# Attention on one core: part of the exponentials moved from ScalarE to a polynomial on VectorE and GpSimd, and the score product split over two row blocks

## The chip, the cores and the metric

The kernel runs on one core of a Trainium2 chip. The metric is the device time of one execution in microseconds (us). Times are compared as medians of several executions of each kernel on the same chip. The names of engines follow the profile: PE is TensorE (PEld its weight loads), DVE is VectorE, ACT is ScalarE, POOL is GpSimd, SP is SyncE.

## The reference: what is computed

The program is a small network of five stages on x of shape 4 x 1024 x 128, all in float32: half a mixture of experts, a selective state-space layer (S6), half a mixture of experts, and the same again with attention in the middle. Only the attention is changed. With 16 heads of 8 columns and 16 "wavelength channels" it computes, cut to what matters:

```python
cos_pm = jnp.cos(phase_modulators)          # 16 channels x 16 heads
def wl_step(acc, wl):
    cpm, iw = wl
    m = cpm[None, :, None, None]
    scores = jnp.einsum('bhqd,bhkd->bhqk', Q * m, K * m) * SCALE
    scores = scores * jnp.cos(KERR * scores * scores)
    attn = jax.nn.softmax(scores, axis=-1)
    out = jnp.einsum('bhqk,bhkd->bhqd', attn, V)
    return (acc + out * iw, None)
...
combined = acc / WL_CHANNELS
```

KERR is 2.7e-12, so the inner cosine is 1 in float32 for scores of this size. A bound on the scores is computed at run time, and the kernel takes the short way (`attention_small`) when it holds, as it does for these inputs. What is left is, for each of 4 batches x 16 heads x 16 channels, exp(c x s) over a 1024 x 1024 matrix s with a factor c per head and channel, then a product with V and a division by the row sums.

## The kernel before, in words

The stages before and after the attention keep x in SBUF (`x_sb`) and run layer norm, experts and S6 over it. S6 (`s6`, lines 226 to 380) is drawn on below only for what its rows show: there DVE runs a scan with two SBUF inputs (L342) and elementwise steps (L313 to L318), while POOL multiplies hst and c_sb (L353) and copies single columns (L351).

`attention` (L527) makes the factors cc and iw from the phase modulators (through `half_sine`), evaluates the bound, and branches to `attention_small` (L594). That function works head by head, 64 heads u in all (4 batches x 16), and 16 channels wl in each, so 1024 channels, numbered g below:

- `batch(b)` normalises and transposes a batch's rows (`xnt`) and makes V with a column of ones (`vts`), so that the row sums come out of the same product.
- `group(n)` makes q and k of four heads (HG = 4) at once, each head on its own block of 32 partitions; row 0 of a block is reserved for the row maxima (q) and ones (k).
- `score(j, a, i, c)` multiplies one 128-row block against all 1024 columns (L712), two matmuls of 512 columns on the head's one block of 32 rows, into a PSUM tile `s` (two buffers).
- `prepare(u)` is a generator of 16 pieces: eight score tiles whose negated maxima go to `nm` (`maxima`, L726), the maxima transposed into the reserved row of q (L734, L741), then eight score tiles in the other orientation, copied to SBUF as `xs` (`head`, L750). With the maxima in the product, `xs` is the shifted score. One piece of the next head but one is advanced per channel.
- The channel loop (L810): one ACTIVATE takes exp of all 8192 columns of `xs` with the channel's factor (L812) into `p_w` (two buffers). PE multiplies it with V in 64 matmuls (L821), in turn on four blocks of output columns, into `o` (two banks). DVE copies `o` to `os` (L829); PE transposes it back (L842); every second channel DVE copies two transposed channels into `ot` (L846).
- `weigh(u, ot)` runs once a head, in the next head's channel 0: reciprocal, weights, product and sum over channels into `comb` (L757 to L770). `out(b)` projects a finished batch in eight pieces (`project`, L508).

The order is written out by hand for PE and DVE (`tc.manual_schedule`, L794): both engines run their instructions in the order in which the loop issues them. The list `beside` says in which channels of which heads the pieces of `group`, `batch` and `out` are issued. ACT and POOL run in the order of issue too. POOL does nothing during the channel loop.

Of the kernel before, what the change touches and what calls it, by code (L numbers as in the profile page):

```python
# [19 lines left out]
F32 = mybir.dt.float32  # L20
# [23 lines left out]
PI2_1 = 6.28125  # L44
PI2_2 = 0.0019350051879882812
PI2_3 = 2.0 * math.pi - PI2_1 - PI2_2
RSQRT = 1597463007.0
LN_TINY = -87.33654

# [468 lines left out]
    nc.vector.tensor_tensor(xt, xt, k.bo, op=ALU.add)  # L518


HG = 4
NG = H // HG
QQ = 4
QW = L // QQ


def attention(tc, k):  # L527
# [8 lines left out]
    with ExitStack() as ctx:  # L536
# [5 lines left out]
        with (  # L542
            tc.tile_pool(name="at_p", bufs=2) as sb,
            tc.tile_pool(name="at_tr", bufs=2, space=PSUM) as ps_tr,
        ):
            z = half_sine(nc, sb, k.pm, H * WL)
            m = sb.tile([P, H * WL], F32, name="m")
            nc.vector.scalar_tensor_tensor(m, z, -2.0, z, op0=ALU.mult, op1=ALU.mult)
            nc.vector.tensor_scalar(m, m, 1.0, None, op0=ALU.add)
            m_hw = m.rearrange("p (w h) -> p h w", h=H)  # L550
            nc.vector.scalar_tensor_tensor(cc, m_hw, SCALE, m_hw, op0=ALU.mult, op1=ALU.mult)
            nc.vector.tensor_scalar(iw, k.iw, 1.0 / WL, None, op0=ALU.mult)

            pb = ps_tr.tile([1, 2, P], F32, name="pb", tag="tr")
            for j, (w_t, b_t) in enumerate(((k.wq, k.bq), (k.wk, k.bk))):
                w2 = sb.tile([C, C], F32, name="w2")
                nc.vector.tensor_tensor(w2, w_t, w_t, op=ALU.mult)
                pn = ps_tr.tile([P, 1], F32, name="pn", tag="pn")  # L560
# [33 lines left out]
def attention_small(tc, k, cc, iw):  # L594
# [10 lines left out]
    with (  # L605
# [5 lines left out]
        tc.tile_pool(name="as_o", bufs=1, space=PSUM) as ps_o,  # L611
    ):

        wp, bp = [], []
        for x, w_t in (("q", k.wq), ("k", k.wk)):
            w = one.tile([C, NG, HG, 32], F32, name=f"wp_{x}")
            nc.gpsimd.memset(w, 0.0)
            nc.gpsimd.tensor_copy(
                w[:, :, :, 1 : 1 + D], w_t.rearrange("c (g j d) -> c g j d", j=HG, d=D)
            )  # L620
            wp.append(w)
            b_t = one.tile([P, NG], F32, name=f"bp_{x}")
            nc.gpsimd.memset(b_t, 0.0)
            if x == "k":
                for j in range(HG):
                    nc.gpsimd.memset(b_t[32 * j : 32 * j + 1, :], 1.0)
            for j in range(HG):
                nc.sync.dma_start(
                    out=b_t[32 * j + 1 : 32 * j + 1 + D, :],
                    in_=k.b_dram[x].rearrange("(g j d) -> j d g", j=HG, d=D)[j],  # L630
                )
            bp.append(b_t)
        nm = one.tile([P, GT], F32, name="nm")
        vts = []
        for j in range(2):
            vt = one.tile([P, GT, H, D + 1], F32, name=f"vt{j}")
            nc.gpsimd.memset(vt[:, :, :, D : D + 1], 1.0)
            vts.append(vt)
        ob = []
# [5 lines left out]
        xnt, qp, kp, comb, xs = {}, {}, {}, {}, {}  # L645

        def batch(b):

# [5 lines left out]
            for half in range(2):  # L654
                pt = ps_t.tile([P, 4, P], F32, name="pt", tag="tr")
                for i in range(4):
                    t = b * GT + half * 4 + i
                    xn = sb.tile([P, C], F32, name="ln_xn", bufs=4)
# [26 lines left out]
        def group(n):  # L685

            for w, b_t, x, at in zip(wp, bp, "qk", (qp, kp)):
                at[n] = sb.tile([P, L], F32, name=f"{x}p")
                for half in range(2):
                    pq = ps_t.tile([P, 512], F32, name="pq", tag="tr")  # L690
                    nc.tensor.matmul(
                        pq,
                        w[:, n % NG].rearrange("c j d -> c (j d)"),
                        xnt[n // NG][:, ts(half, 512)],
                        start=True,
                        stop=True,
# [9 lines left out]

        def score(j, a, i, c):

            row = slice(32 * j, 32 * j + 32)
            s = ps_s.tile([P, L], F32, name="s")  # L710
            for half in range(2):
                nc.tensor.matmul(  # L712
                    s[:, ts(half, 512)],
                    a[row, ts(i, P)],
# [6 lines left out]
        def maxima(u):  # L721

            n, j = divmod(u, HG)
            row = slice(32 * j, 32 * j + 1)
            for i in range(GT):
                nc.vector.tensor_reduce(  # L726
                    nm[:, i : i + 1], score(j, qp[n], i, kp[n]), AX.X, ALU.max, negate=True
                )
                if i < GT - 1:
                    yield  # L730
            for half in range(2):
                pt = ps_t.tile([P, 4, P], F32, name="pt", tag="tr")
                for i in range(4):
                    nc.tensor.matmul(  # L734
                        pt[row, i, :],
                        nm[:, half * 4 + i : half * 4 + i + 1],
                        k.ident,
                        start=True,
                        stop=True,
                    )  # L740
                nc.vector.tensor_copy(  # L741
                    qp[n][row, ts(half, 512)], pt[row].rearrange("p a b -> p (a b)")
                )
            yield

        def head(u):
            n, j = divmod(u, HG)
            xs[u] = xp.tile([P, GT, L], F32, name="xs")
            for i in range(GT):
                nc.vector.tensor_copy(xs[u][:, i, :], score(j, kp[n], i, qp[n]))  # L750
                yield

        def weigh(u, ot):

# [11 lines left out]
            )  # L766

            if h == 0:
                comb[b] = sb.tile([P, 2, QQ, C], F32, name="comb")
# [24 lines left out]
        with tc.manual_schedule(engines={mybir.EngineType.PE, mybir.EngineType.DVE}):  # L794
            finish(batch(0), group(0), prepare(0))
            ahead = prepare(1)
            next(ahead)
            for u in range(n_heads):
                n, j = divmod(u, HG)
                b, h = divmod(u, H)  # L800

                beside = []
                if j == 2 and n + 1 < B * NG:
                    beside.append((10, 14, group(n + 1)))
                if n % NG == 3 and j == 1 and b + 1 < B:
                    beside.append((4, 9, batch(b + 1)))
                if b > 0 and h == 2:
                    beside.append((2, 10, out(b - 1)))
                ot = sb.tile([P, WL, 2 * QQ, D + 1], F32, name="ot", bufs=1)
                for wl in range(WL):  # L810
                    p_w = xp.tile([P, GT, L], F32, name="p_w")
                    nc.scalar.activation(  # L812
                        p_w.rearrange("p a b -> p (a b)"),
                        xs[u].rearrange("p a b -> p (a b)"),
                        AF.Exp,
                        scale=cc[:, h, wl : wl + 1],
                    )
                    o = ob[wl % 2]
                    for i in range(GT):
                        for r in range(QQ):  # L820
                            nc.tensor.matmul(  # L821
                                o[32 * r : 32 * r + D + 1, 0:QW],
                                vts[b % 2][:, i, h, :],
                                p_w[:, i, ts(r, QW)],
                                start=(i == 0),
                                stop=(i == GT - 1),
                            )
                    os = sb.tile([P, QW], F32, name="os")
                    nc.vector.tensor_copy(os, o[:, 0:QW])  # L829
# [5 lines left out]
                    if wl == WL - 1 and u + 2 < n_heads:  # L835
                        finish(ahead)
                        ahead = prepare(u + 2)
                    next(ahead, None)
                    if wl % 2 == 0:
                        pt = ps_t.tile([P, 4, P], F32, name="pt", tag="tr")  # L840
                    for c in range(2):
# [152 lines left out]
def load_attention(nc, pool, k, a):  # L994
# [8 lines left out]
    get(  # L1003
        "pm",
        [P, WL * H],
        a["L1_attn_phase_modulators"].rearrange("w h -> (w h)").partition_broadcast(P),
    )
    get("iw", [P, WL], a["L1_attn_interference_weights"].partition_broadcast(P))


# [93 lines left out]
```

## Time and profile before

| | |
|---|---|
| three timed runs | 8819.01, 8826.69, 8832.57 us; median 8826.69 us |
| profiled execution, its own time | 8833.98 us |
| its span from first to last instruction | 8832.1 us |
| PE busy / PEld busy | 7823.0 / 3392.0 us |
| ACT busy | 7665.0 us |
| DVE busy | 3262.1 us |
| POOL busy | 608.7 us, all before 1400 us |
| granted TensorE clock, mean | 0.918 |
| channel loop, first to last exponential | 1424.5 to 8640.5 us: PE 6531.9, DVE 2224.9, ACT 7167.5 us busy, clock 0.95 |

How to read the lines that follow. A group of the profile's fifth part is a line of the kernel, the engine, the operation, the tile written and the tiles read, their shapes and the number of instructions; then the busy time of all of them in us and the mean of one in ns; then the idle time of the engine just before them and what ended it. A line of the timeline has the start in us, the duration in us, the engine, line, operation, tiles and number of instructions merged into it, and in brackets the idle time before it. Matmuls are pipelined, so their durations overlap: 64 matmuls of 403 ns fill about 4 us. The spans on POOL are rough.

### The profile page before, as it was taken

Reading aid. Unit: us, or ns where it says so; the run is one execution under the profiler, and the core shown is the slowest. Engines: PE = TensorE matmul, PEld = TensorE weight load, DVE = VectorE, ACT = ScalarE, POOL = GpSimd, SP = SyncE. Lnnn points to the kernel's source line nnn. Section 1 sums busy time; section 2 is a strip of 40 time slices with the busy share of each in tenths; the row PEclk is TensorE's granted clock in tenths of the full one; section 3 lists DMA queues with packets and bytes.
Section 4 is the critical chain, followed back from the end, with each engine's and each line's share of the span. In section 5 each row is a group of like instructions: output and inputs, shape, how many; then the busy total and the mean of one; then the engine's idle time right before and its main releaser. Section 6 shows DMA issues by size and latency. Waiting matters only on the chain. (4 is left out here: it accounts for less than half of the span.)

```text
span 8832.1 us, 164134 instructions
## 1 busy us (share of the span) xinstructions
PE 7823.0 (89%) x76474; PEld 3392.0 (38%) x76474; DVE 3262.1 (37%) x5409; ACT 7665.0 (87%) x1746; POOL 608.7 (7%) x579
## 2 busy tenths in 40 slices
PE   8888887999899998989999999999999999899985
PEld 5222253333333333333333333333333333333333
DVE  6777773323333333323233323223333333323222
ACT  3333325999999999999999999999999999999992
POOL 3444430000000000000000000000000000000000
PEclk9777787999999999999999999999999999999996
DMA  0000000000000000000000000000000000000000
GB/s 18 0 0 0 0 6 4 1 1 1 1 1 1 1 1 1 1 1 1 1 1 1 1 1 1 1 1 1 1 1 1 1 1 1 1 1 1 1 1 16
DMA packets 14326, 19.40 MB, mean 2 GB/s; under 512 B 2986, under 2 KB 12722, under 8 KB 13620
## 3 DMA queue, kind: packets, MB, share of 16 engines
q8 instruction: 609, 9.98, 0.5%
q1 hardware_dynamic: 9316, 6.01, 0.2%
q10 hardware_dynamic: 4304, 2.62, 0.1%
q14 instruction: 97, 0.79, 0.0%
HBM read 6.53 MB, written 2.10 MB: 1 GB/s over the span
## 5 line engine op out<-in xcount | busy, mean ns | idle before, releaser
L812 ACT ACTIVATE p_w<-xs,cc 128x8192 f32<-128x8192 f32 x1024 | 7188.6, 7109 | 48.5 <-DVE xs L750 29.1
L821 PE MATMUL o<-p_w,vt 128*9 128x256 f32 x65536 | 4055.1, 403 | 654.3 <-ACT p_w L812 653.4
L821 PEld LDWEIGHTS o<-p_w,vt 128*9 128x9 f32 x65536 | 1809.4, 95 | 2608.2 <-ACT p_w L812 804.3
L829 DVE COPY os<-o 128x256 f32<-128x256 f32 x1024 | 434.9, 425 | 3595.2 <-PE o L821 3595.2
L712 PE MATMUL s<-kp,qp 32*128 32x512 f32 x2048 | 1026.5, 621 | 0.0
L712 PE MATMUL s<-qp,kp 32*128 32x512 f32 x2048 | 1022.1, 619 | 0.0
L750 DVE COPY xs<-s 128x1024 f32<-128x1024 f32 x512 | 627.1, 1225 | 730.4 <-PE s L712 724.3
L726 DVE TENSOR_REDUCE nm<-s 128x1 f32<-128x1024 f32 x512 | 626.2, 1223 | 647.5 <-PE s L712 647.5
L712 PEld LDWEIGHTS s<-qp,kp 32*128 32x128 f32 x2048 | 343.6, 186 | 491.2 <-issue 486.9
L712 PEld LDWEIGHTS s<-kp,qp 32*128 32x128 f32 x2048 | 344.7, 186 | 471.7 <-issue 467.0
L842 PEld LDWEIGHTS pt<-ident,os 128*128 128x128 f32 x2048 | 206.2, 141 | 764.1 <-issue 669.0
L354 PE MATMUL yp<-hm,ident 128*128 128x512 f32 x512 | 388.7, 880 | 99.2 <-POOL hm L353 97.7
L842 PE MATMUL pt<-ident,os 128*128 128x128 f32 x2048 | 450.3, 302 | 19.6 <-DVE os L829 9.6
L336 ACT ACTIVATE da<-delta,neg_a 128x512 f32<-128x512 f32 x256 | 182.7, 721 | 291.9 <-DVE hst L342 291.5
L353 POOL TENSOR_TENSOR hm<-hst,c_sb 128x512 f32<-128x512 f32 x256 | 369.9, 1457 | 166.3 <-ACT c_sb L333 113.3
L178 ACT ACTIVATE r<-hp 128x512 f32<-128x512 f32 x160 | 95.5, 597 | 207.9 <-PE hp L176 185.5
L354 PEld LDWEIGHTS yp<-hm,ident 128*128 128x128 f32 x512 | 110.0, 252 | 348.9 <-POOL hm L353 318.0
L340 DVE TENSOR_TENSOR db<-du,bp 128x512 f32<-128x512 f32 x256 | 164.2, 682 | 152.9 <-PE bp L329 152.0
L333 ACT COPY c_sb<-cp 128x512 f32<-128x512 f32 x128 | 74.8, 585 | 166.1 <-PE cp L331 129.0
L342 DVE TENSOR_TENSOR_SCAN hst<-da,last,db 128x512 f32<-128x512 f32 x128 | 192.0, 1540 | 0.0
L180 POOL TENSOR_TENSOR h<-r 128x512 f32<-128x512 f32 x160 | 164.6, 1047 | 201.7 <-ACT r L178 201.3
L342 DVE TENSOR_TENSOR_SCAN hst<-da,db 128x512 f32<-128x512 f32 x128 | 171.1, 1372 | 5.6 <-POOL hm L353 4.4
(176 smaller groups left out, 3102.8 us busy)
## 6 DMA issues: line engine op xcount, KB each, us to landing
x_sb<-in_L_attn_x_dram ACTq DMA_DIRECT2D x4, 512.0 KB
c_w<-in_L_ffn_w_dram SPq DMA_DIRECT2D x4, 512.0 KB
out_dram<-x_sb SPq DMA_DIRECT2D x4, 512.0 KB
c_w<-in_L_ffn_w_stack_dram SPq DMA_DIRECT2D x1, 512.0 KB
c_w<-in_L_ffn_w_stack_dram ACTq DMA_DIRECT2D x1, 512.0 KB
c_ws<-in_L_ffn_ws_dram SPq DMA_DIRECT2D x2, 128.0 KB
c_w_in<-in_L_attn_W_in_dram SPq DMA_DIRECT2D x1, 256.0 KB
c_w_out<-in_L_attn_W_out_dram SPq DMA_DIRECT2D x1, 128.0 KB
```

Source lines behind the costliest of these rows:

```text
L180: nc.gpsimd.tensor_tensor(h, r, r, op=ALU.mult)
L336: nc.scalar.activation(da, delta[:, c, hc], AF.Exp, scale=neg_a[:, c, n : n + 1])
L342: nc.vector.tensor_tensor_scan(hst, da, db, 0.0 if half == 0 else last[:, c, n : n + 1], op0=ALU.mult, op1=ALU.add,)
L353: nc.gpsimd.tensor_tensor(hm, hst, c_sb, op=ALU.mult)
L354: nc.tensor.matmul(yp[c], k.ident, hm, start=(n == 0), stop=(n == NS - 1))
L712: nc.tensor.matmul(s[:, ts(half, 512)], a[row, ts(i, P)], c[row, ts(half, 512)], start=True, stop=True,)
L726: nc.vector.tensor_reduce(nm[:, i : i + 1], score(j, qp[n], i, kp[n]), AX.X, ALU.max, negate=True)
L750: nc.vector.tensor_copy(xs[u][:, i, :], score(j, kp[n], i, qp[n]))
L812: nc.scalar.activation(p_w.rearrange("p a b -> p (a b)"), xs[u].rearrange("p a b -> p (a b)"), AF.Exp, scale=cc[:, h, wl : wl + 1],)
L821: nc.tensor.matmul(o[32 * r : 32 * r + D + 1, 0:QW], vts[b % 2][:, i, h, :], p_w[:, i, ts(r, QW)], start=(i == 0), stop=(i == GT - 1),)
L829: nc.vector.tensor_copy(os, o[:, 0:QW])
L842: nc.tensor.transpose(pt[:, wl % 2 * 2 + c, :], os[:, ts(c, P)], k.ident)
```

## The change

Four edits in `attention_small`, and some that make room for them.

1. *A polynomial for 512 of the 8192 columns.* The ACTIVATE of a channel takes columns 512 to 8191 only. The first 512 (row block 0, columns 0 to 511) are formed as powers of two: `split(g)` scales the scores and clamps them on DVE, and on POOL rounds them, makes the exponent bits and subtracts (four instructions); `power(g)` evaluates a quintic by five scalar_tensor_tensor on DVE, the last of which multiplies by the exponent bits and writes into `p_w`. The quintic is divided by its top coefficient, and V is multiplied by it for these columns (`vtop`, once a head).
2. *One channel ahead.* In channel g the loop issues split(g + 2), then power(g + 1), after the piece of `prepare`. `p_w` of channel g + 1 is claimed there.
3. *Summed last.* The 64 matmuls of o take row blocks 1 to 7 first and block 0, in which the polynomial's columns lie, last.
4. *Two row blocks a head.* HG is 2: q and k of a head stand twice, on two blocks of 32 partitions, and the two matmuls of a score tile use one block each. The maxima are transposed to 64 rows and added, not copied. `group` now runs every second head and copies its weights on POOL each time (64 such copies).

Beside these, `pm` is loaded when attention starts and not with the other weights; `ln_xn` has one buffer instead of four and `comb` one instead of two; `out` is issued in the first head of the next batch.

```diff
-HG = 4
+HG = 2
+SOFT = 512
...
+            pm = sb.tile([P, WL * H], F32, name="pm", bufs=1)
+            nc.sync.dma_start(
+                out=pm, in_=k.pm_dram.rearrange("w h -> (w h)").partition_broadcast(P)
+            )
...
         def score(j, a, i, c):
-            row = slice(32 * j, 32 * j + 32)
             s = ps_s.tile([P, L], F32, name="s")
             for half in range(2):
+                row = slice(64 * j + 32 * half, 64 * j + 32 * half + 32)
...
+            nc.vector.tensor_copy(nm[:, :, 32], nm[:, :, 0])
...
-                nc.vector.tensor_copy(
-                    qp[n][row, ts(half, 512)], pt[row].rearrange("p a b -> p (a b)")
-                )
+                at = qp[n][rows, ts(half, 512)]
+                nc.vector.tensor_tensor(
+                    at, at, pt[rows].rearrange("p a b -> p (a b)"), op=ALU.add
+                )
...
+        def split(g):
+            u, wl = divmod(g, WL)
+            s, c = xs[u][:, 0, 0:SOFT], cc2[:, u % H, wl : wl + 1]
+            r = sb.tile([P, SOFT], F32, name="x_r")
+            nc.vector.tensor_scalar(r, s, c, -127.0, op0=ALU.mult, op1=ALU.max)
+            p = sb.tile([P, SOFT], F32, name="x_p")
+            nc.gpsimd.tensor_scalar(p, r, 1.0, ROUND, op0=ALU.mult, op1=ALU.add)
+            nc.gpsimd.tensor_scalar(p, p, 1.0, -ROUND, op0=ALU.mult, op1=ALU.add)
+            e = sb.tile([P, SOFT], I32, name="x_e")
+            nc.gpsimd.tensor_scalar(
+                e, p, float(1 << 23), 127.0 * (1 << 23), op0=ALU.mult, op1=ALU.add
+            )
+            nc.gpsimd.tensor_tensor(r, r, p, op=ALU.subtract)
+            return e, r, p
+
+        def power(g, e, r, p):
+            p_w[g] = xp.tile([P, GT, L], F32, name="p_w")
+            nc.vector.scalar_tensor_tensor(p, r, EXP2[4], r, op0=ALU.add, op1=ALU.mult)
+            for c in EXP2[3], EXP2[2], EXP2[1]:
+                nc.vector.scalar_tensor_tensor(p, p, c, r, op0=ALU.add, op1=ALU.mult)
+            nc.vector.scalar_tensor_tensor(
+                p_w[g][:, 0, 0:SOFT],
+                p,
+                EXP2[0],
+                e.bitcast(F32),
+                op0=ALU.add,
+                op1=ALU.mult,
+            )
...
+            power(0, *split(0))
+            parts = split(1)
             for u in range(n_heads):
...
-                if j == 2 and n + 1 < B * NG:
+                if j == 0 and n + 1 < B * NG:
                     beside.append((10, 14, group(n + 1)))
...
+                vtop = sb.tile([P, D + 1], F32, name="vtop")
+                nc.vector.tensor_scalar(vtop, vts[b % 2][:, 0, h], EXP2_TOP, None, op0=ALU.mult)
                 for wl in range(WL):
-                    p_w = xp.tile([P, GT, L], F32, name="p_w")
+                    g = u * WL + wl
                     nc.scalar.activation(
-                        p_w.rearrange("p a b -> p (a b)"),
-                        xs[u].rearrange("p a b -> p (a b)"),
+                        p_w[g].rearrange("p a b -> p (a b)")[:, SOFT:],
+                        xs[u].rearrange("p a b -> p (a b)")[:, SOFT:],
                         AF.Exp,
                         scale=cc[:, h, wl : wl + 1],
                     )
                     o = ob[wl % 2]
-                    for i in range(GT):
+                    for i in (*range(1, GT), 0):
                         for r in range(QQ):
+                            soft = i * L + r * QW < SOFT
                             nc.tensor.matmul(
                                 o[32 * r : 32 * r + D + 1, 0:QW],
-                                vts[b % 2][:, i, h, :],
-                                p_w[:, i, ts(r, QW)],
-                                start=(i == 0),
-                                stop=(i == GT - 1),
+                                vtop if soft else vts[b % 2][:, i, h, :],
+                                p_w[g][:, i, ts(r, QW)],
+                                start=(i == 1),
+                                stop=(i == 0),
                             )
...
                     next(ahead, None)
+                    done, parts = parts, split(g + 2) if g + 2 < n_heads * WL else None
+                    if done:
+                        power(g + 1, *done)
```

In the line numbers of the changed kernel, `split` is L768 to L783, `power` L785 to L798, the ACTIVATE L863 and the matmuls of o L873.

More of the change, by code (lines that the diff above doesn't have):

```diff
@@ L46 @@
 PI2_3 = 2.0 * math.pi - PI2_1 - PI2_2
+LOG2E = 1.4426950408889634
+EXP2 = (753.2121929788568, 522.0867097099356, 180.93752180790148, 41.80864617280965,
+        7.287735181996136)
+EXP2_TOP = 0.0013276472167819944
 RSQRT = 1597463007.0
@@ L545, in attention @@
         ):
-            z = half_sine(nc, sb, k.pm, H * WL)
+            pm = sb.tile([P, WL * H], F32, name="pm", bufs=1)
+            nc.sync.dma_start(
+                out=pm, in_=k.pm_dram.rearrange("w h -> (w h)").partition_broadcast(P)
+            )
+            z = half_sine(nc, sb, pm, H * WL)
             m = sb.tile([P, H * WL], F32, name="m")
@@ L614, in attention_small @@
         wp, bp = [], []
-        for x, w_t in (("q", k.wq), ("k", k.wk)):
-            w = one.tile([C, NG, HG, 32], F32, name=f"wp_{x}")
+        for x in "qk":
+            w = one.tile([C, HG, 2, 32], F32, name=f"wp_{x}")
             nc.gpsimd.memset(w, 0.0)
-            nc.gpsimd.tensor_copy(
-                w[:, :, :, 1 : 1 + D], w_t.rearrange("c (g j d) -> c g j d", j=HG, d=D)
-            )
             wp.append(w)
@@ L623, in attention_small @@
             nc.gpsimd.memset(b_t, 0.0)
[L624 to L627, printed above, removed]
+            for blk in range(4):
+                if x == "k":
+                    nc.gpsimd.memset(b_t[32 * blk : 32 * blk + 1, :], 1.0)
                 nc.sync.dma_start(
-                    out=b_t[32 * j + 1 : 32 * j + 1 + D, :],
-                    in_=k.b_dram[x].rearrange("(g j d) -> j d g", j=HG, d=D)[j],
+                    out=b_t[32 * blk + 1 : 32 * blk + 1 + D, :],
+                    in_=k.b_dram[x].rearrange("(g j d) -> j d g", j=HG, d=D)[blk // 2],
                 )
             bp.append(b_t)
-        nm = one.tile([P, GT], F32, name="nm")
+        nm = one.tile([P, GT, 64], F32, name="nm")
+        nc.gpsimd.memset(nm, 0.0)
         vts = []
@@ L638, in attention_small @@
             vts.append(vt)
+        cc2 = one.tile([P, H, WL], F32, name="cc2")
+        nc.vector.tensor_scalar(cc2, cc, LOG2E, None, op0=ALU.mult)
         ob = []
@@ L643, in attention_small @@
             ob.append(o)
-        xnt, qp, kp, comb, xs = {}, {}, {}, {}, {}
+        xnt, qp, kp, comb, xs, p_w = {}, {}, {}, {}, {}, {}
         def batch(b):
@@ L657, in batch @@
                     t = b * GT + half * 4 + i
-                    xn = sb.tile([P, C], F32, name="ln_xn", bufs=4)
+                    xn = sb.tile([P, C], F32, name="ln_xn", bufs=1)
                     nc.vector.tensor_scalar(
@@ L687, in group @@
             for w, b_t, x, at in zip(wp, bp, "qk", (qp, kp)):
+                nc.gpsimd.tensor_copy(
+                    w[:, :, :, 1 : 1 + D],
+                    (k.wq if x == "q" else k.wk)
+                    .rearrange("c (g j o d) -> c g j o d", j=HG, o=1, d=D)[:, n % NG]
+                    .to_broadcast([C, HG, 2, D]),
+                )
                 at[n] = sb.tile([P, L], F32, name=f"{x}p")
@@ L692, in group @@
                         pq,
-                        w[:, n % NG].rearrange("c j d -> c (j d)"),
+                        w.rearrange("c j h d -> c (j h d)"),
                         xnt[n // NG][:, ts(half, 512)],
@@ L723, in maxima @@
             n, j = divmod(u, HG)
-            row = slice(32 * j, 32 * j + 1)
+            rows = slice(64 * j, 64 * j + 64)
             for i in range(GT):
                 nc.vector.tensor_reduce(
-                    nm[:, i : i + 1], score(j, qp[n], i, kp[n]), AX.X, ALU.max, negate=True
+                    nm[:, i, 0:1], score(j, qp[n], i, kp[n]), AX.X, ALU.max, negate=True
                 )
@@ L734, in maxima @@
                     nc.tensor.matmul(
[L735 to L739, printed above, removed]
-                    )
-                nc.vector.tensor_copy(
-                    qp[n][row, ts(half, 512)], pt[row].rearrange("p a b -> p (a b)")
+                        pt[rows, i, :], nm[:, half * 4 + i, :], k.ident, start=True, stop=True
+                    )
+                at = qp[n][rows, ts(half, 512)]
+                nc.vector.tensor_tensor(
+                    at, at, pt[rows].rearrange("p a b -> p (a b)"), op=ALU.add
                 )
@@ L768, in weigh @@
             if h == 0:
-                comb[b] = sb.tile([P, 2, QQ, C], F32, name="comb")
+                comb[b] = sb.tile([P, 2, QQ, C], F32, name="comb", bufs=1)
             nc.vector.tensor_reduce(
@@ L802, in attention_small @@
                 beside = []
-                if j == 2 and n + 1 < B * NG:
+                if j == 0 and n + 1 < B * NG:
                     beside.append((10, 14, group(n + 1)))
-                if n % NG == 3 and j == 1 and b + 1 < B:
+                if n % NG == NG - 2 and j == 1 and b + 1 < B:
                     beside.append((4, 9, batch(b + 1)))
-                if b > 0 and h == 2:
-                    beside.append((2, 10, out(b - 1)))
+                if b > 0 and h == 0:
+                    beside.append((1, 9, out(b - 1)))
                 ot = sb.tile([P, WL, 2 * QQ, D + 1], F32, name="ot", bufs=1)
+                vtop = sb.tile([P, D + 1], F32, name="vtop")
+                nc.vector.tensor_scalar(vtop, vts[b % 2][:, 0, h], EXP2_TOP, None, op0=ALU.mult)
                 for wl in range(WL):
-                    p_w = xp.tile([P, GT, L], F32, name="p_w")
+                    g = u * WL + wl
                     nc.scalar.activation(
-                        p_w.rearrange("p a b -> p (a b)"),
-                        xs[u].rearrange("p a b -> p (a b)"),
+                        p_w[g].rearrange("p a b -> p (a b)")[:, SOFT:],
+                        xs[u].rearrange("p a b -> p (a b)")[:, SOFT:],
                         AF.Exp,
@@ L1002, in load_attention @@
     k.b_dram = {x: a[f"L1_attn_b{x}"] for x in "qk"}
[L1003 to L1007, printed above, removed]
+    k.pm_dram = a["L1_attn_phase_modulators"]
     get("iw", [P, WL], a["L1_attn_interference_weights"].partition_broadcast(P))
```

## The prediction

> **What bounds the kernel now.** I read the totals and the costliest groups first, then the order of time inside one channel, then the groups of POOL, then two places where engines meet.
>
> ```profile
> span 8832.1 us, 164134 instructions
> ...
> L812 ACT ACTIVATE p_w<-xs,cc 128x8192 f32<-128x8192 f32 x1024 | 7188.6, 7109 | 48.5 <-DVE xs L750 29.1
> L821 PE MATMUL o<-p_w,vt 128*9 128x256 f32 x65536 | 4055.1, 403 | 654.3 <-ACT p_w L812 653.4
> ...
> L829 DVE COPY os<-o 128x256 f32<-128x256 f32 x1024 | 434.9, 425 | 3595.2 <-PE o L821 3595.2
> ```
>
> 1024 exponentials fill 7188.6 us and wait 48.5 in all, so ScalarE sets the pace of attention. Its instructions run from 1424.5 to 8640.5 us: 7216 us, **7.05 us a channel**. The other 1616 us (layer norms, experts, S6) are touched only by small set-up edits; 1.9 us lie outside the span (profiled time 8833.98, 7.3 above the median of the runs, 8826.69).
>
> One channel in the timeline (start, duration, engine, line):
>
> ```profile
> 5005.41 1.98 PE L712 MATMUL s<-qp,kp 32*128 32x512 f32 x4
> 5005.55 0.42 DVE L829 COPY os<-o 128x256 f32<-128x256 f32 x1 [2.75 <-PE o L821]
> ...
> 5007.43 1.22 DVE L750 COPY xs<-s 128x1024 f32<-128x1024 f32 x1 [1.46 <-PE s L712]
> ...
> 5008.68 5.14 PE L821 MATMUL o<-p_w,vt 128*9 128x256 f32 x64 [0.93 <-ACT p_w L812]
> ```
>
> After channel g's o, PE makes one score tile (1.98 us), then DVE drains it (1.22). DVE then idles until the next o ends. Nothing in this string feeds the next exponential at once; it has a whole channel of slack.
>
> **What the change removes.** 512 of 8192 columns leave each ACTIVATE. L336's 128x512 takes 721 ns, L812's 128x8192 7109: 0.832 ns a column, so 0.43 us a channel, 436 us in all, and a pace of 6.62 if ScalarE stays the bound. The score tile's two halves move to two row blocks. Where head 0's tile (rows 0 to 31) met head 1's (rows 32 to 63), before the loop, the trace shows what that gives:
>
> ```profile
> 1419.79 1.21 PE L712 MATMUL s<-kp,qp 32*128 32x512 f32 x1
> 1419.98 1.05 PE L712 MATMUL s<-qp,kp 32*128 32x512 f32 x1
> ```
>
> The two tiles' matmuls run side by side. A tile should cost 1.1 us (half of 1.98 plus the drain) instead of 1.98; bounds 1.1 and 2.0.
>
> **What it adds, and where.** In the built program DVE's order in channel g becomes: os(g), score drain, r(g+2), five scalar_tensor_tensor of power(g+1), os(g+1). The last of the five writes the block that the last eight matmuls of o(g+1) wait for; os(g+1) and the next score tile stand behind those on DVE and PE. So a **ring** closes each channel: end of o(g), score, drain, r, power, end of o(g+1). The exponential runs up to a channel ahead and doesn't relax it. The pace is the larger of 6.62 and the ring.
>
> Uncontended: score 1.1; drain 0.04 + 1.22; r 0.43 (L313, a tensor_scalar of 1024, took 669 to 694 ns, L473's of 256 took 296); five power steps at 0.69 (L133, 128x512 with two inputs, 686 ns) and 0.03 between, 3.6; tail 0.74 (64 matmuls took 3.6 at full clock, so eight 0.43, plus 0.23 of latency, and 0.08 from a release to the first matmul, as from the exponential's end at 5008.60). Sum 7.1.
>
> What was hidden and now stands on the ring: per head, weigh (0.94 + 0.29 + 1.22 + 2.08 less 1.0 beside the score tile, 3.5), the maxima's copy, transposes and two adds (0.16 + 0.7 + 2 x 0.69 by L734 and L741, 2.3), per two heads four group steps (0.86 on PE and L698's 0.75 less what overlaps, about 1.0 each; there are twice as many groups), batch and out (20 steps of about 2.5 and 32 of about 2.2, each a short walk between DVE and PE: 120 us over the run), vtop 0.2. Over 16 channels 0.62. The uncontended ring is **7.7 us**, above 7.05 already.
>
> **The port.** POOL does four steps of split(g+2) exactly while DVE does power(g+1): both start from r's end. Both read SBUF. The S6 stage shows such a meeting (DVE's step with two SBUF inputs against POOL's product):
>
> ```profile
> 919.20 1.26 POOL L353 TENSOR_TENSOR hm<-hst,c_sb 128x512 f32<-128x512 f32 x1
> 919.24 2.30 DVE L314 SCALAR_TENSOR_TENSOR sp_z<-sp_w,sp_z 128x1024 f32<-128x1024 f32 x1
> ```
>
> L314 is the kind of step that power adds. Beside hm it took 2.30 us, in four of its eight runs 1.23: it waited to hm's end and then needed 1.08. POOL waits alike: of 256 hm, 54 that began inside a scan took 1.06 from the scan's end against 1.26 alone, and the copy of one column stretched from 0.17 to 1.14. The Trainium skill, "SBUF — State Buffer", section "Who interferes with whom", says that a DVE instruction with two SBUF inputs and a GpSimd one that reads SBUF exclude each other for the whole instruction. Row and rule disagree on price: by the rule as stated the nine steps add in full (with T, below, 0.8 before its wait: 3.45 + 1.26 + 2.4 = 7.1 us); by the rows each step that waited is 0.15 (DVE) or 0.20 (POOL) shorter after it. I take the rows. Since each POOL step waits for its forerunner, as DVE's do, the two alternate: 0.69 + 4 x 0.54 + 1.06 for the subtraction + 3T + 8 hand-overs of 0.03 = 4.15 + 3T.
>
> T, a POOL tensor_scalar of 512 with one input, after its wait, is in no row. Near it:
>
> ```profile
> L180 POOL TENSOR_TENSOR h<-r 128x512 f32<-128x512 f32 x160 | 164.6, 1047 | 201.7 <-ACT r L178 201.3
> ...
> L617 POOL MEMSET wp_q<- 128x512 f32 x1 | 0.5, 524 | 70.3 <-DVEq L582 70.3
> ...
> L618 POOL COPY wp_q<-c_wq 128x128 f32<-128x128 f32 x1 | 0.3, 309 | 0.0
> ```
>
> The copy reads one input: (309 - 100)/128 = 1.63 ns a column over about 0.1 fixed (the memsets of a few columns), 0.94 at 512, 0.74 after a wait. "GPSIMD Engine Reference", section "Engine selection", has one-input work at roughly line rate, which speaks for the change: the memset's 0.52 shows that rate, 0.35 after a wait (an estimate). The ring part is 5.2 by the rule and 6.4 by the row; the ceiling is the two-input cost, 1.06, giving 7.3. I take T = 0.6, nearer the row, since that copy writes runs of eight: 5.95 in place of 3.6.
>
> Ring: 1.1 + 1.26 + 0.43 + 5.95 + 0.74 + 0.62 = **10.1 us**.
>
> **Clock.** PE was granted 0.95 over the loop and busy 6.53 of 7.22 ms; its work would be 5.2 us in 10. From 1400 to 1434 us, with PE on score tiles alone, the grant was half. At half speed score and tail grow by 1.65 us a channel; bounds 0 and 1.65. I take a quarter, 0.4: **10.5 us**.
>
> **Small edits.** pm now loads when attention starts (L473 waited 1.5 us for it; 0 to 5 us once). One ln_xn buffer instead of four ties each transpose to the next (in the 120 us). Weight copies on POOL, 64 of about 0.3, queue between the splits and delay a group step by that, under 20 us. An extra copy of nm, 0.16 a head, is in the 2.3. Total: 1616 + 1.9 + 1024 x 10.5 + 20 = 12,390; I say **12,400 us**.
>
> **Rivals.**
> (a) Alternation as above, 0.76: from T = 0.35 with full clock (9.4: 11,250) to T = 1.06 with the clock mostly low (about 12.0: 13,900).
> (b) The two meet only in part, about half of the 2.4 us, because POOL gets ahead or its steps are short, 0.12: ring 8.9, 10,750. For it: no row shows four POOL steps against five of DVE. Against: both wait for their own forerunner and start together.
> (c) No exclusion for these forms: ring 7.7, 9,520; 0.07. Against: L314 is the same form.
> (d) The other side, 0.05: ScalarE stays the bound at 6.62, 1616 + 2 + 6779 + 20 = 8,420. Mechanism: the ring closes inside the shorter exponential, since power's dependent steps overlap in DVE and POOL's fall beside the drain, which reads PSUM. It decides where the ring is below 7.05; the uncontended sum is 0.65 above that, and below 6.62 the full gain appears. If the score tile also failed to shorten, the ring would gain another 0.9.
>
> That the polynomial's work isn't done as said isn't open: the instructions stand in the program.
>
> **Numbers.** Likeliest 12,400. Range 10,500 to 13,800: it takes in most of (a) and the greater part of (b), and leaves out (c), (d), the foot of (b) and the top of (a), about 0.2. A measurement can tell about 0.2% from no change. Faster by more 0.05 (d), within 0.01, slower 0.94.
>
> **What would show it.** ACT idle before L863 of about 3.5 us a channel, released by PE o; power's steps (L788 to L791) with means near 1.1 us instead of 0.69; POOL's L776 to L782 stretched likewise; PE waiting for p_w L791 inside each o; score tiles near 1.1 us. Wrong if L790 means 0.69 (then (c)), if ACT's idle stays under 0.1 us a channel (then (d)), or if L776's own time is far from 0.6.

## The result, and the profile after

| | before | changed |
|---|---|---|
| median (range) of 4 runs each | 8822.85 us (8812.24 to 8832.57) | 11696.75 us (11682.87 to 11707.53) |
| ratio, 95% interval | | 1.3257 (1.3234 to 1.328) |
| profiled execution: own time, span | 8833.98, 8832.1 | 11691.15, 11689.3 |
| first to last exponential of the channel loop | 7237 us, 7.07 a channel | 10,106 us, 9.87 a channel |
| outside the loop | 1595 us | 1583 us |
| granted TensorE clock in the loop | 0.95 | 0.83 |

The change makes the kernel a third slower, and all of the difference, 2869 us, lies in the loop over the channels. (The loop of before really ends at 8661.5 us. The 8640.5 of the prediction, and of the table of before, was 21 us short, so the prediction's "outside" was 21 too large.)

The groups of the changed kernel's page, with the same columns as before:

```profile
L863 ACT ACTIVATE p_w<-xs,cc 128x7680 f32<-128x7680 f32 x1024 | 6855.9, 6699 | 3250.1 <-PE o L873 2886.8
...
L776 POOL TENSOR_SCALAR x_p<-x_r 128x512 f32<-128x512 f32 x1024 | 1014.1, 990 | 5148.6 <-DVE x_r L774 5144.5
L790 DVE SCALAR_TENSOR_TENSOR x_p<-x_p,x_r 128x512 f32<-128x512 f32 x3072 | 3014.5, 981 | 106.4
...
L791 DVE SCALAR_TENSOR_TENSOR p_w<-x_p,x_e 128x512 f32<-128x512 f32 x1024 | 1601.4, 1564 | 109.3 <-DVE x_p L790 2.3
L782 POOL TENSOR_TENSOR x_r<-x_r,x_p 128x512 f32<-128x512 f32 x1024 | 1634.9, 1597 | 65.0
...
L788 DVE SCALAR_TENSOR_TENSOR x_p<-x_r 128x512 f32<-128x512 f32 x1024 | 700.3, 684 | 3.5 <-POOL x_r L782 3.5
```

ScalarE did give up its 512 columns (7109 to 6699 ns), but where it waited 48.5 us in all, it now waits 3250, 3.2 a channel, and 2887 of them until PE's o. L788, L790 and L791 are one kind of instruction on tiles of one size: the first of a power takes 684 ns, the next three 981, the last 1564. POOL's L782 takes 1597 ns where a product of two such tiles (L353 of before) took 1260 alone.

The list of waits says who holds whom (waiting engine, total us, times, longest):

```profile
ACT p_w L863 <- PE o L873: 2886.8, 896, 11.6
PE o L873 <- DVE p_w L791: 2723.1, 958, 8.2
```

The exponential waits for o, because o frees its `p_w`; o waits for the last step of the polynomial.

One ordinary channel in the timeline of the changed kernel, at full TensorE clock (the lines left out are of PE and ScalarE, and copies off this path):

```profile
5999.37 0.68 DVE L788 SCALAR_TENSOR_TENSOR x_p<-x_r 128x512 f32<-128x512 f32 x1
5999.55 0.99 POOL L776 TENSOR_SCALAR x_p<-x_r 128x512 f32<-128x512 f32 x1 [3.48 <-DVE x_r L774]
...
6000.09 3.02 DVE L790 SCALAR_TENSOR_TENSOR x_p<-x_p,x_r 128x512 f32<-128x512 f32 x3
...
6000.62 0.93 POOL L777 TENSOR_SCALAR x_p<-x_p 128x512 f32<-128x512 f32 x1
...
6001.64 0.93 POOL L779 TENSOR_SCALAR x_e<-x_p 128x512 int32<-128x512 f32 x1
...
6002.63 1.60 POOL L782 TENSOR_TENSOR x_r<-x_r,x_p 128x512 f32<-128x512 f32 x1
6003.21 1.57 DVE L791 SCALAR_TENSOR_TENSOR p_w<-x_p,x_e 128x512 f32<-128x512 f32 x1
...
6004.83 0.39 PE L873 MATMUL o<-p_w,vtop 128*9 128x256 f32 x2 [1.36 <-DVE p_w L791]
...
6005.38 1.13 PE L729 MATMUL s<-qp,kp 32*128 32x512 f32 x4
...
6006.56 1.22 DVE L765 COPY xs<-s 128x1024 f32<-128x1024 f32 x1 [0.61 <-PE s L729]
...
6007.70 0.48 DVE L774 TENSOR_SCALAR x_r<-xs,cc 128x512 f32<-128x512 f32 x1
...
6008.09 0.68 DVE L788 SCALAR_TENSOR_TENSOR x_p<-x_r 128x512 f32<-128x512 f32 x1
```

Read it twice. Down the DVE lines, from one L788 to the next, 8.72 us pass: power 5.41 (to L791's end at 6004.78), tail 0.60 (PE's last eight matmuls of o, to the score tile's start), score 1.18 (to the start of L765), drain 1.14 (L765 copies the tile out of PSUM), r 0.39 (L774). Across engines, from L788 on, the ends alternate between DVE and POOL, although the durations overlap. I read each POOL step's duration as its wait for a DVE step and then its own work, and each DVE step's as the reverse: L791 ends 0.55 us after L782, having begun 1.02 before that end.

### The profile page after: what moved, and what is told of

It is laid out like the page before. It is cut to its first block, busy times and chain, and to the rows that moved or that the text cites. A ratio compares the mean times of both kernels' runs of the same rounds, so it can differ in the third digit from the quotient of the medians.

```text
span 11689.3 us, 174952 instructions
## 1 busy us (share of the span) xinstructions
PE 8336.9 (71%) x76602; PEld 3192.8 (27%) x76602; DVE 8964.9 (77%) x11746; ACT 7332.0 (63%) x1746; POOL 5183.1 (44%) x4738
## 5 line engine op out<-in xcount | busy, mean ns | idle before, releaser
L863 ACT ACTIVATE p_w<-xs,cc 128x7680 f32<-128x7680 f32 x1024 | 6855.9, 6699 | 3250.1 <-PE o L873 2886.8
L873 PE MATMUL o<-p_w,vt 128*9 128x256 f32 x61440 | 4819.0, 446 | 7.7 <-ACT p_w L863 7.7
L776 POOL TENSOR_SCALAR x_p<-x_r 128x512 f32<-128x512 f32 x1024 | 1014.1, 990 | 5148.6 <-DVE x_r L774 5144.5
L790 DVE SCALAR_TENSOR_TENSOR x_p<-x_p,x_r 128x512 f32<-128x512 f32 x3072 | 3014.5, 981 | 106.4
L873 PE MATMUL o<-p_w,vtop 128*9 128x256 f32 x4096 | 723.1, 436 | 2888.0 <-DVE p_w L791 2723.1
L873 PEld LDWEIGHTS o<-p_w,vt 128*9 128x9 f32 x61440 | 1754.9, 103 | 2202.1 <-issue 1293.0
L791 DVE SCALAR_TENSOR_TENSOR p_w<-x_p,x_e 128x512 f32<-128x512 f32 x1024 | 1601.4, 1564 | 109.3 <-DVE x_p L790 2.3
L782 POOL TENSOR_TENSOR x_r<-x_r,x_p 128x512 f32<-128x512 f32 x1024 | 1634.9, 1597 | 65.0
L873 PEld LDWEIGHTS o<-p_w,vtop 128*9 128x9 f32 x4096 | 110.7, 90 | 3399.7 <-DVE p_w L791 3202.6
L777 POOL TENSOR_SCALAR x_p<-x_p 128x512 f32<-128x512 f32 x1024 | 956.1, 934 | 84.5
L779 POOL TENSOR_SCALAR x_e<-x_p 128x512 int32<-128x512 f32 x1024 | 955.6, 933 | 84.6
L765 DVE COPY xs<-s 128x1024 f32<-128x1024 f32 x512 | 627.1, 1225 | 443.8 <-PE s L729 443.8
L788 DVE SCALAR_TENSOR_TENSOR x_p<-x_r 128x512 f32<-128x512 f32 x1024 | 700.3, 684 | 3.5 <-POOL x_r L782 3.5
L774 DVE TENSOR_SCALAR x_r<-xs,cc 128x512 f32<-128x512 f32 x1024 | 489.1, 478 | 0.9
```

The costliest lines, as they stand in the source:

```text
L776: nc.gpsimd.tensor_scalar(p, r, 1.0, ROUND, op0=ALU.mult, op1=ALU.add)
L777: nc.gpsimd.tensor_scalar(p, p, 1.0, -ROUND, op0=ALU.mult, op1=ALU.add)
L779: nc.gpsimd.tensor_scalar(e, p, float(1 << 23), 127.0 * (1 << 23), op0=ALU.mult, op1=ALU.add)
L782: nc.gpsimd.tensor_tensor(r, r, p, op=ALU.subtract)
L788: nc.vector.scalar_tensor_tensor(p, r, EXP2[4], r, op0=ALU.add, op1=ALU.mult)
L790: nc.vector.scalar_tensor_tensor(p, p, c, r, op0=ALU.add, op1=ALU.mult)
```

## The experiments

Theory: a ring (o, score tile, drain, r, power, o) sets the pace, and in it DVE's five steps alternate with POOL's four because the two exclude each other. The rivals were a ring without exclusion (the steps are simply long, or the added waits cost), the TensorE clock, and the fourth edit (two row blocks) or the extra waits as causes of their own. "Pace" is the loop divided by 1024. "Ordinary" is the commonest distance from one channel to the next, without the pieces that come once or a few times a head; in the changed kernel 387 channels are so, and another 167 take about 10.1 us, with a score tile of 2.08 us at a low clock. Every "of before" is against the kernel before in the same session; its medians lay between 8823.57 and 8829.26 us.

### 1. POOL's four steps only write

```diff
-            nc.gpsimd.tensor_scalar(p, r, 1.0, ROUND, op0=ALU.mult, op1=ALU.add)
-            nc.gpsimd.tensor_scalar(p, p, 1.0, -ROUND, op0=ALU.mult, op1=ALU.add)
+            nc.gpsimd.memset(r, 0.25)
+            nc.gpsimd.memset(p, 0.0)
...
-            nc.gpsimd.tensor_scalar(e, p, ...)
-            nc.gpsimd.tensor_tensor(r, r, p, op=ALU.subtract)
+            nc.gpsimd.memset(e.bitcast(F32), 1.0)
+            nc.gpsimd.memset(r, 0.25)
```

> The changed kernel with POOL's four steps of split replaced by four memsets of the same tiles, the first on r, so that they still start at r's end and DVE's power steps still wait for the last of them; the rounding, the exponent bits and the subtraction are left out. Theory (DVE's steps with two SBUF inputs and POOL's steps that read SBUF exclude each other): a memset reads nothing, so L790 falls from 981 to about 690 ns and L791 from 1564 to about 690, the power part from 5.4 to 3.6 us, the pace from 9.87 to about 7.9 us a channel, the time to about 9,700 us. Rival (any POOL work beside DVE stretches it, writing included): L790 stays above 850 ns, the time above 10,700. Rival (the stretching isn't on the ring): no change, 11,700.

Measured: 9670.63 us, 1.0957 (1.094 to 1.0974) of before; pace 7.89, ordinary 6.97. The same stretch in its timeline:

```profile
6006.08 0.68 DVE L786 SCALAR_TENSOR_TENSOR x_p<-x_r 128x512 f32<-128x512 f32 x1
6006.23 0.52 POOL L776 MEMSET x_r<- 128x512 f32 x1 [3.11 <-DVE x_r L774]
6006.80 2.15 DVE L788 SCALAR_TENSOR_TENSOR x_p<-x_p,x_r 128x512 f32<-128x512 f32 x3
6006.81 0.53 POOL L780 MEMSET x_r<- 128x512 f32 x1
6009.05 0.69 DVE L789 SCALAR_TENSOR_TENSOR p_w<-x_p,x_e 128x512 f32<-128x512 f32 x1
```

Two memsets lie inside power, and neither side gets longer: 0.52 and 0.53 for POOL, 2.15 for three steps of DVE. Power takes 3.66 us from the first start to the last end instead of 5.41. So the stretch needs POOL's reads, not POOL's being busy. That an instruction of GpSimd that only writes doesn't contend with a two-input one of DVE is also what the Trainium skill states ("SBUF — State Buffer", "Who interferes with whom"). The other two memsets came after power and POOL's steps were shorter too, so this run bounds the exclusion but doesn't isolate it; the next one does.

### 2. The same work in another order: power first, then split

```diff
-                    done, parts = parts, split(g + 2) if g + 2 < n_heads * WL else None
-                    if done:
-                        power(g + 1, *done)
+                    if parts:
+                        power(g + 1, *parts)
+                    parts = split(g + 2) if g + 2 < n_heads * WL else None
```

> The changed kernel with power(g+1) issued ahead of split(g+2), so that POOL's steps run beside the tail of o, the score tile and the drain, which have one SBUF input at most. Theory (exclusion plus ring): L790 and L791 near 690 ns; but POOL's chain, about 3.3 us from r's end, now ends about 0.9 us after the drain, so DVE waits there for POOL: ring 7.5 us at full clock, with heads and clock about 8.2, time about 10,000 us. Rival (the sum of DVE's and POOL's work is in series whatever the order): above 11,200. Rival (the stretching is all there is): 1.9 + 0.5 us off the ring and no new wait, 9,300.

Measured: 9991.68 us, 1.1312 (1.1295 to 1.1329); pace 8.21, ordinary 7.56. From its groups:

```profile
L790 DVE SCALAR_TENSOR_TENSOR x_p<-x_p,x_r 128x512 f32<-128x512 f32 x3072 | 2126.3, 692 | 104.8
...
L788 DVE SCALAR_TENSOR_TENSOR x_p<-x_r 128x512 f32<-128x512 f32 x1024 | 705.3, 689 | 504.1 <-POOL x_r L782 502.0
...
L776 POOL TENSOR_SCALAR x_p<-x_r 128x512 f32<-128x512 f32 x1024 | 635.6, 621 | 4979.8 <-DVE x_r L774 4975.7
```

Not one instruction is taken away, and 1705 us go. POOL now works beside o, score and drain. L790 falls from 981 to 692 ns, L791 from 1564 to 692; POOL's tensor_scalar falls from 990 to 621 and its product from 1597 to 1283. It is the meeting that costs, not the steps. What is left of the loss has another cause, in the ordinary channels of this run:

```profile
6053.66 0.69 DVE L788 SCALAR_TENSOR_TENSOR x_p<-x_r 128x512 f32<-128x512 f32 x1 [0.89 <-POOL x_r L782]
...
6061.23 0.69 DVE L788 SCALAR_TENSOR_TENSOR x_p<-x_r 128x512 f32<-128x512 f32 x1 [0.90 <-POOL x_r L782]
```

Power now waits 0.9 us for POOL, as was expected: r, POOL's four steps and power close a second ring, and it sets the 7.56 us.

### 3. Only the fourth edit and the small ones

```diff
-            power(0, *split(0))
-            parts = split(1)
...
-                        p_w[g].rearrange("p a b -> p (a b)")[:, SOFT:],
-                        xs[u].rearrange("p a b -> p (a b)")[:, SOFT:],
+                        p_w[g].rearrange("p a b -> p (a b)"),
+                        xs[u].rearrange("p a b -> p (a b)"),
...
-                    for i in (*range(1, GT), 0):
+                    for i in range(GT):
```

> The kernel before with the fourth edit and the small ones alone (two row blocks a head, 32 groups, pm and buffers), no polynomial: ScalarE takes all 8192 columns. Theory: ScalarE stays the bound with 7.02 us of work a channel, everything else hides: pace 7.05 to 7.10, time within 0.5% of before, though a score tile falls from 2.0 to about 1.2 us. Rival (the extra groups, adds and POOL copies reach the path): 1 to 2% slower, 8,900 to 9,000. Rival (the lighter PE shortens today's waits): up to 0.5% faster, 8,780.

Measured: 8803.58 us, 0.9969 (0.9958 to 0.9981). One of the two score groups before, then here, and PE's wait for the exponential here:

```profile
L712 PE MATMUL s<-kp,qp 32*128 32x512 f32 x2048 | 1026.5, 621 | 0.0
...
L729 PE MATMUL s<-kp,qp 32*128 32x512 f32 x2048 | 582.9, 645 | 0.7 <-DVE nm L743 0.7
...
L837 PE MATMUL o<-p_w,vt 128*9 128x256 f32 x65536 | 4060.0, 404 | 1285.6 <-ACT p_w L828 1285.6
```

A group is 512 tiles: two row blocks do shorten the tile, from 2.0 to 1.14 us, 883 us over both groups. But PE had slack: its wait for the exponential grows from 653.4 us to 1285.6, which takes up 632 of them, and the kernel gains 0.3%. So none of the slowdown is this edit's, nor that of one `ln_xn` buffer, the later `pm` or the weight copies.

### 4. PE kept busy with 40 idle matmuls a channel

```diff
+                        for d in range(40 if i == 0 else 0):
+                            nc.tensor.matmul(
+                                o[32 * (d % QQ) : 32 * (d % QQ) + D + 1, 0:QW],
+                                none,
+                                p_w[g][:, 1, ts(d % QQ, QW)],
+                                start=False,
+                                stop=False,
+                            )
```

`none` is a tile of zeros, so o is unchanged; the 40 stand ahead of the last eight matmuls of o.

> The changed kernel with 40 more matmuls a channel, of zero weights on the same exponentials, between the 56 and the last eight of o; they add zero. Theory (the granted clock, 0.83 in the loop, lengthens score tile and tail, which lie on the ring): PE, busy through its wait, is granted 0.95 or more, a channel falls to the 8.7 to 8.8 us seen where the clock is full, pace about 9.3 with the heads' pieces, time about 11,100 us. Rival (the clock costs nothing, or the filler delays the last eight): 11,700 or above, up to 12,500.

Measured: 11921.77 us, 1.3504 (1.3483 to 1.3524). It missed: slower than the changed kernel, not 5% faster.

```profile
6004.94 4.50 PE L874 MATMUL o<-p_w,none 128*9 128x256 f32 x80
...
6007.04 1.59 DVE L793 SCALAR_TENSOR_TENSOR p_w<-x_p,x_e 128x512 f32<-128x512 f32 x1
...
6009.26 0.39 PE L883 MATMUL o<-p_w,vtop 128*9 128x256 f32 x2
```

The clock rose as meant, to 0.98 in the loop, but each of the 40 stands in the trace twice (x80), they fill 4.50 us, to 6009.44 by the modelled ends, and the last eight start 0.63 us after power's end at 6008.63 instead of 0.05 after it. The filler had become part of the ring: ordinary 9.31, which is 8.72 and those 0.6. The run says nothing of the clock's price, so I repeated it with half as many.

### 5. 20 idle matmuls a channel

```diff
-                        for d in range(40 if i == 0 else 0):
+                        for d in range(20 if i == 0 else 0):
```

> As e4 with 20 more matmuls instead of 40. In e4 each of the 40 stood twice in the trace and took 4.5 us together, so the last eight came 0.6 us after power's end; 20 take 2.25 us and end before it. Theory (clock alone): an ordinary channel takes 8.72 us throughout, the pace is that of e4 less its delay of 0.59, 9.5 us, the time about 11,330 us, 3% under the changed kernel. Rival (the clock's share is covered elsewhere, or the filler still delays): 11,600 to 11,900.

Measured: 11356.12 us, 1.2859 (1.2837 to 1.288), as expected. The clock is 0.93 in the loop, nearly that of before (0.95), and the ordinary channel takes 8.72 through most of the loop.

```profile
6004.00 0.39 PE L883 MATMUL o<-p_w,vtop 128*9 128x256 f32 x2 [1.38 <-DVE p_w L793]
...
6009.01 2.34 PE L874 MATMUL o<-p_w,none 128*9 128x256 f32 x40
```

The filler now ends ahead of power and PE waits 1.38 us for it as in the changed kernel. Pace 9.55: the low clock is worth at least 9.87 - 9.55 = 0.32 us a channel, some 330 us of the 2870. It is a consequence of the ring (PE waits, and is granted less), not the cause.

### 6. Power two channels ahead, split three

```diff
             power(0, *split(0))
-            parts = split(1)
+            power(1, *split(1))
+            parts = split(2)
...
-                    done, parts = parts, split(g + 2) if g + 2 < n_heads * WL else None
-                    if done:
-                        power(g + 1, *done)
+                    if parts:
+                        power(g + 2, *parts)
+                    parts = split(g + 3) if g + 3 < n_heads * WL else None
```

> As e2, and power runs one channel earlier still: in channel g the loop issues power(g+2), then split(g+3). Theory (a ring closes through PE because o(g+1) needs a power that DVE can only start after o(g)): with power(g+2) needed by o(g+2) alone, the ring is open and DVE's own work sets the pace: os 0.42, drain 1.22, power 3.55, r 0.48, transposed channels 0.15, heads 0.45 = 6.3 us, plus about 1.5 of waiting for POOL's chain of 3.3 us, 7.8: about 9,600 us. Rival (the ring isn't the reason, DVE and POOL together are): like e2 within 1%. Rival (POOL's chain hides): ScalarE's 6.6 us, 8,400.

Measured: 9840.31 us, 1.1155 (1.1137 to 1.1172); pace 8.06. That is 1.5% under experiment 2 and 2.5% above what the theory gave: nearly the rival. o no longer waits for power, and yet little is gained:

```profile
6010.09 0.62 POOL L776 TENSOR_SCALAR x_p<-x_r 128x512 f32<-128x512 f32 x1 [7.20 <-DVE x_r L774]
...
6012.18 1.29 POOL L782 TENSOR_TENSOR x_r<-x_r,x_p 128x512 f32<-128x512 f32 x1
6013.50 0.69 DVE L788 SCALAR_TENSOR_TENSOR x_p<-x_r 128x512 f32<-128x512 f32 x1 [1.31 <-POOL x_r L782]
...
6016.48 0.69 DVE L791 SCALAR_TENSOR_TENSOR p_w<-x_p,x_e 128x512 f32<-128x512 f32 x1
6017.08 0.48 DVE L774 TENSOR_SCALAR x_r<-xs,cc 128x512 f32<-128x512 f32 x1
```

What is left is the second ring: r, POOL's four (3.38), power (3.67), next r: 7.56 us, whatever PE and ScalarE do, because in this order split(g+3) stands behind power(g+2) on DVE and power behind POOL. L788 waits 1558.9 us in all for POOL's L782. Experiment 2 had stood at the same 7.56, so opening the first ring could gain little; my theory counted 1.5 us of waiting for POOL, but didn't see that this ring alone sets the pace.

Could 512 columns gain in another order? When the steps alternate, power's 5.41 us, os (0.42), drain (1.14) and r (0.39) fill 7.4 us of DVE a channel; with power first the second ring takes 7.56. Both are above the 7.07 of before. From this I argue that 512 columns are too many, but I have not tried every order.

### 7 and 8. 256 columns, in the new order and in the old

```diff
-SOFT = 512
+SOFT = 256
```

Experiment 7 is experiment 6 with this line:

> As e5 with 256 columns by the polynomial in place of 512. Theory: a power step falls to about 0.43 us and POOL's chain to about 2.0, which then fits beside os and drain; DVE's work is 4.8 us a channel and ScalarE's 7936 columns set the pace at 6.82: about 8,600 us, 2.5% under the kernel before. Rival (clock and heads' pieces still reach the path): 8,800 to 9,000.

Experiment 8 is the changed kernel with this line alone:

> The changed kernel with SOFT = 256 and nothing else. Theory (the ring is a sum that shrinks with the columns): the alternation falls from 5.4 to about 2.7 us and r by 0.15, so that an ordinary channel's ring is 5.9 us at full clock, below ScalarE's 6.82; with heads' pieces and the clock the pace is about 6.9 to 7.1: 8,650 to 8,850 us. Rival (fixed costs of the nine steps weigh more than the columns): ring above 7.5, over 9,250 us.

Measured: 7 takes 8623.97 us, **0.9775 (0.9761 to 0.9788)**, the best of all kernels here. 8 takes 8774.11 us, 0.9944 (0.993 to 0.9958). First of 7, then of 8:

```profile
L864 ACT ACTIVATE p_w<-xs,cc 128x7936 f32<-128x7936 f32 x1024 | 6970.7, 6898 | 72.9 <-PE o L874 30.5 <-issue 24.1 <-ACT p_w L864 12.8
...
L790 DVE SCALAR_TENSOR_TENSOR x_p<-x_p,x_r 128x256 f32<-128x256 f32 x3072 | 1306.4, 425 | 105.3
```

```profile
L863 ACT ACTIVATE p_w<-xs,cc 128x7936 f32<-128x7936 f32 x1024 | 6983.0, 6900 | 208.9 <-PE o L873 174.8 <-DVE xs L765 31.2
...
L790 DVE SCALAR_TENSOR_TENSOR x_p<-x_p,x_r 128x256 f32<-128x256 f32 x3072 | 1539.6, 501 | 105.5
...
L791 DVE SCALAR_TENSOR_TENSOR p_w<-x_p,x_e 128x256 f32<-128x256 f32 x1024 | 785.1, 767 | 109.1 <-DVE x_p L790 3.2
```

In both, ScalarE is the bound again. In 8 the steps still stretch (501 and 767 ns against 425) but the ordinary ring, about 6.1 us, is now shorter than the exponential's 6.8, and ScalarE idles 208.9 us: 131 of them before a head's first, fourth and fifth exponential, around the weighing, and 53 before its ninth and tenth, after the maxima's transposes. In 7 the steps don't stretch, and it idles 72.9. 256 columns are worth 218 us (0.832 ns each, 1024 times). 7 is about 200 us under before and 8 about 50, and in both some 25 of these may be the other edits' (experiment 3). The sign of the change hangs on which of ring and exponential is longer.

### 9 and 10. The halves back on one row block

```diff
-                row = slice(64 * j + 32 * half, 64 * j + 32 * half + 32)
+                row = slice(64 * j, 64 * j + 32)
```

Experiment 9 is the changed kernel with this line:

> The changed kernel with both halves of a score tile on the head's first row block, the fourth edit undone where it counts. Theory: the score tile, now on the ring, goes back from 1.1 to 2.0 us at full clock and from 2.1 to 3.8 at half: pace 10.8 to 10.9, time about 12,700 us. Rival (os and weigh cover the score tile): under 12,000. The clock could take part of it back, since PE is busier.

Experiment 10 is experiment 7 with it:

> As e6 (256 columns, power two channels ahead) with both halves of a score tile on one row block. Theory (with the ring open the score tile no longer lies on the path): ScalarE still sets 6.80 us; PE has 2.0 + 0.44 + 3.6 = 6.1 us a channel at full clock and fits: within 0.7% of e6, 8,620 to 8,690. Rival (PE, near 90% busy, becomes the bound through its waits): above 8,750.

Measured: 9 takes 12809.29 us, 1.4512 (1.449 to 1.4535); 10 takes 8726.44 us, 0.9879 (0.9862 to 0.9895). The score tile of 9 and the exponential of 10:

```profile
6007.07 1.98 PE L729 MATMUL s<-kp,qp 32*128 32x512 f32 x4
...
L864 ACT ACTIVATE p_w<-xs,cc 128x7936 f32<-128x7936 f32 x1024 | 6979.0, 6898 | 152.2 <-PE o L874 71.1
```

In the ring, a score tile of 1.98 us instead of 1.13 makes the ordinary channel 9.56 instead of 8.72, and with a lower clock (0.80) the kernel 1110 us slower. So the fourth edit, worth 0.3% by itself, is worth 9% once it stands on the ring. In 10, where ScalarE is the bound, it still costs about 1.1%, between theory and rival. The profiled executions of 10 and 7 are 113 us apart (8740.85 and 8627.64): 79 are further idle time of ScalarE (152.2 against 72.9) and 29 come before the loop, whose first exponential starts at 1444.9 instead of 1416.1.

## Why the prediction came out as it did

The sum, term by term, in us a channel; the measured ones are from the ordinary channel above, and from experiment 5 for the last two:

| term | predicted | measured |
|---|---|---|
| score and drain | 1.1 + 1.26 | 1.18 + 1.14 |
| r | 0.43 | 0.39 |
| power alternating with split | 5.95 | 5.41 |
| tail | 0.74 | 0.60 |
| pieces of a head, spread | 0.62 | 9.55 - 8.72 = 0.83 |
| clock | 0.4 | 9.87 - 9.55 = 0.32 |
| pace | 10.5 | 9.87 |

- *The ring and the order of DVE.* Right: the chain stands in the timeline as predicted, and breaking it by order alone (experiments 2 and 6) or by size (7, 8) takes most of the loss away.
- *The exclusion and the alternation.* Right. The formula 4.15 + 3T gives the measured 5.41 with T = 0.42. Experiments 1 and 2 exclude rival (c): without POOL's reads beside it, a step is 692 ns. Experiment 2 keeps the added waits too, so they are not what stretched the steps. Rival (b), a partial meeting, fell too: the nine steps pass one by one. On the price the rows were right and the rule as the prediction took it was not (the section's words on the whole instruction stand at DVE's two-port modes): added in full, at what each takes alone in experiment 2, the nine steps make 5 x 0.69 + 3 x 0.62 + 1.28 = 6.6 us, and they took 5.41.
- *T, the mis-sized term.* I chose 0.6 "nearer the row", the copy of L618, against the Trainium skill's line rate ("GPSIMD Engine Reference", "Engine selection"). Experiment 2 has POOL's tensor_scalar at 0.621 us alone for 512 columns, experiment 7 at 0.407 for 256: 0.84 ns a column over about 0.19. After a wait, 0.2 shorter, that is 0.42. The rule was much nearer than the row: by its end, 0.35, the alternation would be 5.2, by mine 5.95, measured 5.41. The copy writes runs of eight and was a poor stand-in; 3 x 0.18 x 1024 = 553 us of the 703 by which 12,400 overshot are this.
- *Tail.* 0.14 too long, 143 us. PE starts the last eight 0.05 after power's end, and the score tile 0.55 after that.
- *Pieces of a head.* 0.21 too short, 215 us the other way. In experiment 5 the first channel of a head, with the weighing and vtop, takes 4.2 us more than 8.72 in the mean (predicted 3.5 and 0.2). The seventh, with the maxima's copy, transposes and adds, takes 4.6 more, where 2.3 were predicted: this piece was mis-sized most. In one such channel the second add ends 4.63 us after the copy begins, because it waits for 16 transposes that alone fill 3.7:

```profile
4561.59 0.18 DVE L750 COPY nm<-nm 128x8 f32<-128x8 f32 x1
4561.81 3.68 PE L754 MATMUL pt<-ident,nm 128*64 128x128 f32 x16 [1.54 <-DVE nm L750]
...
4565.53 0.69 DVE L758 TENSOR_TENSOR qp<-qp,pt 64x512 f32<-64x512 f32 x1 [1.02 <-PE pt L754]
```

- *Clock.* 0.4 taken, 0.32 found: the grant fell to 0.83, and a score tile took 2.08 us where it was low. Experiment 5 doesn't take all of that away: the channel after the weighing still takes 1.4 us more than 8.72 there, with such a tile. That is 0.09 a channel which the table counts under the pieces, so the clock is nearer 0.41 and the pieces nearer 0.74.
- *Small edits.* Experiment 3 shows none of the 20 us taken for them, and the first step that reads `pm` waited 0.2 us for it.
- *Rival (d)*, that ScalarE stays the bound, failed because the ring isn't under 6.62. Its condition was right: at 256 columns the ring is shorter than the exponential, and the time falls below before.
- *The predicted signs.* ScalarE idle 3.2 us a channel, 2.8 of them by PE's o (predicted 3.5); means of the five steps (684 + 3 x 981 + 1564)/5 = 1038 ns (predicted near 1.1 us), but unequal: the first isn't delayed, since POOL starts after it, and the last bears the long subtraction.

## What to carry to other kernels

Work taken off the bounding engine is free only if what replaces it doesn't close a ring with the consumer: write down the order on each in-order engine, add up one turn of the ring and compare it with the bound, instead of comparing busy shares (here DVE was 77% busy, PE 71% and ScalarE 63%, and a ring through DVE and PE was the bound).
Two chains of dependent steps on DVE and GpSimd that both read SBUF, two inputs on DVE's side, ran in turn, step by step, when they started together; put them at different times (1705 us here for three lines moved), and cost them as one resource when choosing the size.
A removed stall is worth what the next ring allows: with the meeting gone, r, POOL and power made a ring of 7.56 us by themselves, and freeing o from power as well gained only another 1.5%.

## What the runs showed of the hardware that was not expected

- GpSimd's one-input tensor_scalar in f32 took 0.621 us for 128x512 and 0.407 for 128x256, about half of the two-input product (1.28 and 0.73).
- The clock granted to TensorE followed how it was fed: 0.83 in the loop of the changed kernel, 0.93 with 20 idle matmuls a channel and 0.98 with 40. But while PE was mostly on score tiles of 32 rows before the loop, busy 25.8 of 34 us, it was granted 0.51 in the kernel before.
- Of the filler matmuls each stood twice in the trace, 80 for 40, in 4.50 us. That is 0.056 us a record, as much as one of the kernel's own takes (56 in 3.21 us), so the time speaks for each having run twice; why, no run shows.
